# A fused recurrent layer on one core: the first loads of x, the issue of two weights, and fewer warm-up passes

## The chip, the cores and the metric

The kernel runs on one core of a Trainium2 chip. The metric is device time in microseconds (us) from launch to the end of the program; lower is better. Five engines work side by side, each with its own instruction stream: PE (TensorE, matrix products), DVE (VectorE), ACT (ScalarE), POOL (GpSimd) and SP (SyncE, which here only issues DMAs). ACT and POOL issue some DMAs too. DMA transfers run on 16 DMA engines that all issuing engines share.

## The reference

The input x has 8 sequences of 1024 tokens with 256 channels, in float32. Each sequence is normalised and goes through two branches whose results are added to x:

```python
xn = _layernorm(x, axis=-1)
x = x + hawk(xn, Wg, Wi, conv_w, conv_b, lru_Wi, lru_bi, lru_Wg, lru_bg, lam, Wo) \
      + channel_mix(xn, W_r, W_k, W_v, mu_r, mu_k)

def hawk(x, ...):                       # hidden size 384
    gate = x @ Wg.T
    u    = x @ Wi.T
    y    = causal_conv4(u, conv_w) + conv_b
    ig   = sigmoid(y @ lru_Wi.T + lru_bi)
    rg   = sigmoid(y @ lru_Wg.T + lru_bg)
    alpha = exp(-8 * softplus(lam) * rg)
    xbeta = sqrt(1 - alpha**2 + 1e-6) * ig * y
    h    = scan(h = alpha * h + xbeta)   # along the tokens
    return (gelu(gate) * h) @ Wo.T

def channel_mix(x, ...):
    x_prev = shift_one_token(x)
    xr = mu_r * x + (1 - mu_r) * x_prev
    xk = mu_k * x + (1 - mu_k) * x_prev
    return sigmoid(xr @ W_r) * (square(relu(xk @ W_k)) @ W_v)
```

## The kernel before

The sequences are worked one after the other, with the scan and the last product of one sequence laid between the products of the next. Tokens lie 128 to a tile, so a sequence has TT = 8 tiles (`xt`, tokens on partitions). PE needs the normalised x with channels on partitions (`xnT`). Most products use a seven-product scheme of the Strassen kind, for which POOL builds sums of weight blocks (`weight_sum`, line 408: `sum_u`, `sum_r`, `sum_k` and others) and sums of token blocks (`token_sum`, line 803). `w_u` holds two weights side by side, Wi (`"i"`, rows for u) and Wg (`"g"`, rows for the gate); the first sum of `w_u` waits for both.

The order of the instructions on every engine is written out by hand: a list of steps with due times (`PLACES`, `at`, `pe`) is sorted once and issued in that order, and each engine takes its instructions strictly in order. What this case is about is what stands ahead of that list, the head for the first sequence. Tiles of x are treated in four pairs, f = 0 to 3:

- The loads of x are issued by SP, two tiles in each DMA (`load`, line 707). After the second of them stand three instructions of ACT: the DMA of Wi (`load_weight`, line 349), the DMA of the small parameters `par`, and the load of the table for the square root. After the four loads SP issues Wg and the other weights (W_k, W_r, the two of the recurrence, W_v, Wo).
- `busy(15)` (line 1025) gives PE fifteen products of zeros, 128 x 512 in bfloat16, whose results nobody reads. They are first in PE's order. Two more such passes follow the first transposes.
- For each pair, DVE computes the statistics (`bn_stats` line 725, `bn_aggr` line 729); ACT the square root (`deviation`, line 732); DVE a reciprocal and a small product (lines 739 and 740); then ACT normalises one tile of the pair (line 749) and DVE the other (line 747).
- PE transposes the pair (`early_transposes`, line 1044) and ACT copies the result to `xnT` (`early_put`, line 1057). Between the transposes PE computes quarters of the first products with Wi (`plain_quarters`, line 581): per pair f a quarter for each of two output rows, four matmuls of 256 columns each in the records. The order on PE is: passes, transposes 0, two passes, quarter (0, first row), transposes 1, quarter (0, second row), quarter (1, first row), transposes 2, quarters, transposes 3, quarters.
- On ACT the square root of pair 1 stands behind the copy of pair 0, and so on; on DVE the statistics of pair 1 stand behind the normalising of pair 0, and the statistics of pair 2 ahead of the reciprocal of pair 1.

After the quarters come the products of line 415, which belong to the main scheme and to all later sequences.

A DMA's landing is counted on one of eight counters, which the build hands out in turn over the DMAs of SP and ACT. A DMA can be issued only when the one eight places ahead of it has landed. In the kernel before, W_r takes the counter of Wi.

Of the kernel before, what the change touches and what calls it, by code (L numbers as in the profile page):

```python
# [9 lines left out]
AF = mybir.ActivationFunctionType  # L10
# [231 lines left out]
def kernel(  # L242
# [24 lines left out]
    nc = tc.nc  # L267
    B, S, D = x.shape
    TT = S // P
# [6 lines left out]
    def fixed(name, shape, dtype=F32):  # L276
        return const.tile([P] + shape, dtype, tag=name, name=name)


    par = fixed("par", [COLS])  # L280
# [57 lines left out]
    def take():  # L338
        return free.pop(0)

    def give(b):
        free.append(b)
# [4 lines left out]
    def load_weight(engine, name, src):  # L347
        family, first = ROWS[name]
        engine.dma_start(families[family][:, :, first * P : first * P + src.shape[2]], src)
# [356 lines left out]
    def load(s, t, n):  # L706
        nc.sync.dma_start(
            xt[:, t : t + n, :],
            x[s, t * P : (t + n) * P, :].rearrange("(t p) d -> p t d", p=P),
        )  # L710
# [8 lines left out]
    def stats(s, t, n):  # L719
        sums_of_tiles(s, t, n)  # L720
        moments(s, t, n)
# [279 lines left out]
    with tc.manual_schedule():  # L1001
# [1 line left out]
        nc.gpsimd.memset(ln_eps, LN_EPS)  # L1003
        nc.gpsimd.memset(beta_eps, BETA_EPS)
        make_identity(nc, ident)
        for t in range(0, TT, 2):
            load(0, t, 2)
            if t == 2:
                load_weight(nc.scalar, "i", w_i)
                nc.scalar.dma_start(par, params)  # L1010
                nc.scalar.preload_act_table(AF.Sqrt)
        load_weight(nc.sync, "g", w_g)
        load_weight(nc.sync, "k", w_k)
        load_weight(nc.sync, "r", w_r)
        load_weight(nc.sync, "lg", lru_wg)
# [6 lines left out]
        def busy(n):  # L1022
            for _ in range(n):
                b = take()
                nc.tensor.matmul(banks[b], warm[:, 0:P], warm, start=True, stop=True)  # L1025
                give(b)
# [40 lines left out]
                mu_rest, par[:, COL_MU_R : COL_MU_K + DC], -1.0, 1.0, ALU.mult, ALU.add  # L1067
            )

        busy(15)  # L1070
        stats(0, 0, 2)
        scales(0, 2)
        early_normalize(0)
# [289 lines left out]
```

## Time and profile before

| | us |
|---|---|
| median of three runs (620.11 to 620.37) | 620.17 |
| the profiled execution's own time | 620.45 |
| its span, first to last instruction | 618.7 |
| PE busy in the span | 613.3 (99%) |
| DVE, ACT, POOL busy | 532.0, 472.7, 320.2 |
| span's part ahead of the first product of line 415 | 18.2 |

A busy PE is counted from the start of a matmul to its modelled end; matmuls overlap, so the spacing of their starts says how fast they go. Times in the views count from the span's start.

### The profile page before, as it was taken

To read this page: it belongs to the slowest core of one execution; us is meant where nothing else is said; L and a number is where in the kernel's file an instruction comes from. 1 tells how busy PE (TensorE), PEld (TensorE's weight loads), DVE (VectorE), ACT (ScalarE), POOL (GpSimd) and SP (SyncE) were. 2 spreads that over 40 slices of the span, in tenths; PEclk is the share of its full clock that TensorE was granted. 3 is DMA by queue.
4 is the path that set the end of the run, shared out by engine and by line. 5 is a ranking of instruction groups with operands and counts; after the bars stand their busy time and mean duration, and the time that the engine had idled before them with its cause. 6 is when DMAs were issued, how large, how long until landed. Compare 5 with 4: busy or idle time off the path is not lost.

```text
span 618.7 us, 7488 instructions
## 1 busy us (share of the span) xinstructions
PE 613.3 (99%) x2539; PEld 370.0 (60%) x2539; DVE 532.0 (86%) x659; ACT 472.7 (76%) x671; POOL 320.2 (52%) x227
## 2 busy tenths in 40 slices
PE   8999999999999999999999999999999999999998
PEld 4575445954469544794448844497445964457466
DVE  5789799999989798898899888998888986789696
ACT  4988998668894788938889398884888749884880
POOL 4977923579034950549407492084911769427000
DMA  7200600164001810029000480006500044000403
GB/s 272 69 1 8 129 0 1 27 179 69 0 1 48 195 31 0 1 69 205 0 1 1 102 171 0 2 3 151 120 0 1 17 120 69 0 0 1 69 17 119
DMA packets 35478, 35.10 MB, mean 57 GB/s; under 512 B 2800, under 2 KB 34928, under 8 KB 35440
## 3 DMA queue, kind: packets, MB, share of 16 engines
q1 hardware_dynamic: 26416, 25.63, 14.9%
q0 software_dynamic: 8320, 8.39, 9.1%
q10 hardware_dynamic: 704, 0.60, 0.3%
q8 instruction: 20, 0.33, 0.2%
q14 instruction: 18, 0.15, 0.1%
HBM read 19.94 MB, written 8.39 MB: 46 GB/s over the span
## 4 chain that ended last, share of the span: by engine, by line
PE 96%; DVE 3%; issue 0%; ACT 0%; DVEq 0%
PE bank L415 65%; PE bank L421 24%; PE bank L830 4%; PE bank L1025 1%; PE bank L581 1%; DVE xr L820 1%; DVE xt L747 0%; DVE bank L499 0%; DVE st L725 0%; PE bank L754 0%; DVE q L915 0%; PE bank L1044 0%; DVE mv L740 0%; DVE q L930 0%; DVE mv L729 0%
## 5 line engine op out<-in xcount | busy, mean ns | idle before, releaser
L415 PE MATMUL bank<-y,w_l 128*128 128x512 f32 x288 | 138.2, 593 | 0.1
L898 DVE SCALAR_TENSOR_TENSOR y<-u,par,y 128x1024 f32<-128x1024 f32 x72 | 111.6, 1573 | 0.2
L491 ACT COPY bank<-bank 128x512 f32<-128x512 f32 x76 | 43.8, 576 | 61.3 <-PE bank L415 45.3
L415 PEld LDWEIGHTS bank<-y,w_l 128*128 128x128 f32 x288 | 52.9, 190 | 59.2 <-issue 56.9
L499 DVE TENSOR_TENSOR bank<-bank,five 128x512 f32<-128x512 f32 x76 | 52.3, 689 | 26.4 <-PE bank L415 25.6
L415 PE MATMUL bank<-ysum,sum_l 128*128 128x512 f32 x144 | 71.1, 594 | 0.2
L415 PE MATMUL bank<-xsum,sum_u 128*128 128x512 f32 x138 | 69.3, 592 | 0.0
L803 POOL TENSOR_TENSOR tr<-g 128x512 f32<-128x512 f32 x12 | 22.0, 1836 | 83.7 <-ACT u L611 69.8
L803 POOL TENSOR_TENSOR ysum<-y,ysum 128x512 f32<-128x512 f32 x16 | 28.4, 1777 | 53.6 <-DVE y L898 51.1
L803 POOL TENSOR_TENSOR xsum<-ysum 128x512 f32<-128x512 f32 x12 | 16.0, 1347 | 66.0 <-PE bank L421 58.8
L415 PEld LDWEIGHTS bank<-ysum,sum_l 128*128 128x128 f32 x144 | 26.8, 190 | 35.3 <-issue 28.7
L496 ACT COPY five<-bank 128x512 f32<-128x512 f32 x76 | 43.6, 583 | 4.9 <-PE bank L415 2.9
L415 PE MATMUL bank<-xnT,w_u 128*128 128x512 f32 x92 | 47.0, 592 | 0.0
L623 ACT ACTIVATE tr<-bank,half_b 128x512 f32<-128x512 f32 x48 | 32.0, 679 | 15.6 <-PE bank L415 15.6
L415 PEld LDWEIGHTS bank<-xsum,sum_u 128*128 128x128 f32 x138 | 25.7, 190 | 29.7 <-issue 27.5
L421 PE MATMUL bank<-w_o,g 128*128 128x128 f32 x288 | 37.0, 275 | 0.0
L623 ACT ACTIVATE ti<-bank,half_b 128x512 f32<-128x512 f32 x48 | 31.5, 683 | 7.1 <-PE bank L415 6.9
L421 PEld LDWEIGHTS bank<-w_o,g 128*128 128x128 f32 x288 | 35.0, 192 | 2.9 <-issue 2.9
L749 ACT ACTIVATE xt<-xt,mv,std 128x256 f32<-128x256 f32 x60 | 33.9, 596 | 1.5 <-DVE mv L740 1.5
L922 DVE SCALAR_TENSOR_TENSOR ti<-ti,y 128x1024 f32<-128x1024 f32 (+1 forms) x25 | 29.9, 1216 | 3.9 <-ACT ti L623 3.9
L803 POOL TENSOR_TENSOR ysum<-y 128x512 f32<-128x512 f32 x16 | 20.4, 1273 | 23.8 <-DVE y L898 20.1
L925 DVE SCALAR_TENSOR_TENSOR ti<-ti,q 128x1024 f32<-128x1024 f32 (+1 forms) x25 | 31.8, 1272 | 0.7
(165 smaller groups left out, 1480.3 us busy)
## 6 DMA issues: line engine op xcount, KB each, us to landing
side<-in_x_dram POOLq DMA_DIRECT2D x8, 1024.0 KB, 9.3
xt<-in_x_dram SPq DMA_DIRECT2D x28, 256.0 KB, 5.1
xnT<-xk SPq DMA_DIRECT2D x96, 64.0 KB, 2.0
out_dram<-side SPq DMA_DIRECT2D x12, 512.0 KB, 4.8
xt<-in_x_dram SPq DMA_DIRECT2D x1, 1024.0 KB, 5.3
out_dram<-side SPq DMA_DIRECT2D x4, 256.0 KB, 2.2
out_dram<-side SPq DMA_DIRECT2D x6, 128.0 KB, 1.8
w_l<-in_lru_wg_dram SPq DMA_DIRECT2D x1, 576.0 KB, 5.8
```

The source lines that it names most:

```text
L415: nc.tensor.matmul(banks[b], weight, tokens, start=start, stop=True, skip_group_check=True)
L421: nc.tensor.matmul(banks[b][:, p], tokens[:, p], weight, start=start and j == 0, stop=True, skip_group_check=True,)
L491: nc.scalar.copy(banks[bank["B"]], banks[bank["A"]])
L496: nc.scalar.copy(self.five, banks[bank["C"]])
L499: nc.vector.tensor_tensor(banks[bank["C"]], banks[bank["B"]], self.five, ALU.add)
L623: nc.scalar.activation(dst[:, m, HALVES[h]], src, AF.Tanh, bias=half_b[:, b + m : b + m + 1], scale=0.5)
L749: nc.scalar.activation(xa, xa, AF.Identity, bias=m, scale=r)
L803: nc.gpsimd.tensor_tensor(dst[o], a, b, ALU.subtract)
L830: nc.tensor.matmul(banks[b][:, j * D : (j + 1) * D], lhs[:, c, (t + j) * P : (t + j + 1) * P], families[w][:, c, :], start=(j == 0 and c = ...
L898: nc.vector.scalar_tensor_tensor(y[:, m, :], u[:, m, k : k + S], column(COL_CONV_W + k * HC + m), y[:, m, :], ALU.mult, ALU.add,)
L922: nc.vector.scalar_tensor_tensor(ti[:, m, p], ti[:, m, p], 1.0, y[:, m, p], ALU.add, ALU.mult)
L925: nc.vector.scalar_tensor_tensor(ti[:, m, p], ti[:, m, p], 0.5, q[:, m, p], ALU.mult, ALU.mult)
```

## The change

Three edits, all in the head. First, x's tiles 0 and 1 are loaded by one DMA each instead of one for both, and the other three pairs as before, so that SP issues five loads of x in place of four. Second, ACT issues Wi and then Wg, and after them `par` and the table load; SP no longer issues Wg. Third, ten passes of zeros in place of fifteen.

The order of all other instructions on every engine stays as it was. With one DMA more ahead of them, the counters shift: W_k now takes the counter of Wi, W_r that of the load of tile 0.

```diff
@@ -1003,13 +1003,14 @@
         nc.gpsimd.memset(ln_eps, LN_EPS)
         nc.gpsimd.memset(beta_eps, BETA_EPS)
         make_identity(nc, ident)
-        for t in range(0, TT, 2):
+        load(0, 0, 1)
+        load(0, 1, 1)
+        load_weight(nc.scalar, "i", w_i)
+        for t in range(2, TT, 2):
             load(0, t, 2)
-            if t == 2:
-                load_weight(nc.scalar, "i", w_i)
-                nc.scalar.dma_start(par, params)
-                nc.scalar.preload_act_table(AF.Sqrt)
-        load_weight(nc.sync, "g", w_g)
+        load_weight(nc.scalar, "g", w_g)
+        nc.scalar.dma_start(par, params)
+        nc.scalar.preload_act_table(AF.Sqrt)
         load_weight(nc.sync, "k", w_k)
         load_weight(nc.sync, "r", w_r)
         load_weight(nc.sync, "lg", lru_wg)
@@ -1067,7 +1068,7 @@
                 mu_rest, par[:, COL_MU_R : COL_MU_K + DC], -1.0, 1.0, ALU.mult, ALU.add
             )
 
-        busy(15)
+        busy(10)
         stats(0, 0, 2)
         scales(0, 2)
         early_normalize(0)
```

## The prediction

> **What bounds the kernel now.** I read the page's engine shares first, then busy times by stretch, then the chain of waits over the first 19 us, then the DMA answers and the engines' rows there. By stretch (length, then busy time of PE, PEld, DVE, ACT, POOL):
>
> ```profile
> 18.20:107.00 88.80, 88.65 (x295) 47.56 (x294) 78.39 (x114) 80.78 (x117) 59.54 (x45) 1.00 0.16 33
> 107.00:152.00 45.00, 44.75 (x233) 29.97 (x232) 43.43 (x53) 31.50 (x46) 33.05 (x21) 1.00 0.43 94
> 152.00:610.00 458.00, 458.00 (x1926) 278.21 (x1925) 397.51 (x456) 350.79 (x493) 218.04 (x140) 1.00 0.23 49
> ```
>
> From 18.2 us on PE is idle for 0.4 of 591.8 us. The change touches nothing there, so its worth is the shift of the first product of line 415, which starts at 18.19. The chain ahead of it (start, length, what):
>
> ```profile
> 1.18 5.96 PE bank L1025 x15
> 7.14 0.45 PE bank L1044 x4
> ...
> 8.10 0.31 ACT std L732
> ...
> 8.82 0.98 DVE xt L747
> ...
> 10.70 0.94 DVE mv L740
> ...
> 11.79 1.06 DVE xt L747
> 12.85 0.04 issue
> 12.90 0.55 PE bank L1044 x3
> 13.44 1.81 PE bank L581 x8
> ```
>
> The fifteen passes hold the first transposes, whose copy stands on ACT ahead of pair 1's square root at 8.10. From there the chain is DVE's normalising of pairs 1 and 2; from 12.90 PE never waits again. Those DVE steps are long for a reason that their neighbours show:
>
> ```profile
> 5.02 0.16 DVE L740 SCALAR_TENSOR_TENSOR mv<-mv,std 128x2 f32<-128x2 f32 x1
> 5.22 0.41 DVE L747 TENSOR_SCALAR xt<-xt,std,mv 128x256 f32<-128x256 f32 x1
> 8.65 2.01 POOL L408 TENSOR_TENSOR sum_u<-w_u 128x384 f32<-128x384 f32 x2 [7.21 <-DMA w_u<-in_w_g_dram]
> ```
>
> L740 takes 0.16 and L747 0.41 with POOL idle, but 0.94 and 0.98 to 1.06 while POOL's sums of w_u run (8.65 to 12.7, four of 1.0 each): DVE's step ends about where POOL's does. POOL starts when Wg lands.
>
> **The loads of x and the weights.** DMA queues between 3.0 and 3.7 us (q1 is SP's, q10 ACT's; packets, MB, share), and three issues (KB, us to landing) of Wi at 0.73, of x's second pair at 1.23, of Wg at 2.75:
>
> ```profile
> q10 hardware_dynamic: 159, 0.24, 101.1%
> q1 hardware_dynamic: 3, 0.00, 0.2%
> ...
> w_u<-in_w_i_dram ACTq DMA_DIRECT2D x1, 384.0 KB, 4.5
> xt<-in_x_dram SPq DMA_DIRECT2D x1, 256.0 KB, 4.7
> w_u<-in_w_g_dram SPq DMA_DIRECT2D x1, 384.0 KB, 5.8
> ```
>
> The DMA engines are full. Though x's second pair was issued at 1.23, only Wi moves: the first pair, then Wi, then the second pair. Whether this is turn-taking between the queues or order of issue, the changed kernel's order comes out the same: tile 0, Wi, tile 1, Wg, pair 1, par, pair 2, pair 3. The rate: from Wi's landing (0.73 + 4.5 = 5.2) to Wg's (2.75 + 5.8 = 8.5), 1166 KB (three pairs, par, Wg) in 3.3 us, 353 KB/us. I count bytes from Wi's landing, with 640 KB before it:
>
> - tile 1 completes the same 640 KB: 5.2; before, both tiles were there at 0.73 + 2.7 = 3.4;
> - Wg, 1024 KB: 6.3 (before 8.5); pair 1, 1280 KB: 7.0 (before 5.9); pair 2, 1550 KB: 7.8 (6.7); pair 3, 1806 KB: 8.5 (7.4).
>
> The Trainium skill's page DMA: Bandwidth & Descriptors, section Issuing engines are not separate DMA queues, speaks against the change: it says that DMAs from different issuers share the same engines and interleave, so a second issuer saves only issue time. By it Wg on ACT takes its time from x, as counted here; a reader who instead thinks of ACT's queue as separate would get pair 1 at its old 5.9.
>
> Issuing itself: SP has one load more (0.5 us; four took 1.98) and is rid of Wg (0.69). W_k must now wait for Wi's landing (4.9) instead of going at 3.48; W_r, the recurrence's weights, W_v and Wo stand behind it, W_v besides for Wg, Wo for pair 2. The engines have x and Wg to move until 8.5 anyway, so W_k and W_r land as before, near 9.2 and 9.9; POOL reads them after 10.5. ACT's Wg issue (0.65, like Wi's) pushes par to 2.1 and the 1.28 us table load to 2.75 to 4.03; the first square root comes later than that (4.49 before, 5.9 below). Cost of both: nothing.
>
> **Pair 0.** Before, statistics began at 3.42 and the square root came 1.07 later. With tile 0's done (0.37), it is 0.70 after 5.2: 5.9. As before, +0.33 to the reciprocal and +0.20 to L740: 6.45. POOL starts 0.15 after Wg: also 6.45, with sums of w_u to 10.5. No row shows which goes first when they start together. If DVE does, only L747 is held: pair 0 is ready at 7.5. If POOL does, L740 ends at 7.4, and L747, which follows behind a new sum, at 8.5. Before it was 5.82. I take 8.5, by the row at 10.70, where POOL was 0.08 ahead and DVE waited; 7.5 is the other end.
>
> **Pairs 1 and 2.** Statistics of pair 1 follow on DVE at 8.5; square root 1.07 later, 9.6, also behind pair 0's copy (9.0 to 9.55). L740 at 10.1 waits for POOL's fourth sum to 10.4; L747 then meets POOL's short sums of W_r and W_k (0.45 each) and ends at 11.0. Before it was 9.80. With pair 0 at 7.5: square root 8.6, L740 held to 9.45, L747 to 10.5. Pair 2: from 9.80 to 12.84 was 3.04, 1.49 of them waiting for POOL (0.78 in L740, 0.71 in L747); with short sums I put 0.4: 11.0 + 1.95 = 12.95.
>
> **PE.** From pair 1's readiness: transposes done 0.45 later, two quarters of 0.86, then transposes 2 of 0.44. Before: 9.80 to 11.97, then idle 0.93, and done at 13.28. Changed: 11.0 + 0.45 + 1.72 = 13.17, where pair 2 (12.95) is ready, done at 13.61: **0.33 later**. With pair 1 at 10.5: 13.11, 0.17 earlier. So most of pair 1's lateness goes into PE's old idle time, and the five passes removed (2.1 us) gain nothing, since PE then waits for x: what is late next is tile 1. POOL's first sum over xnT, which waited 0.70 for the last copy, moves with PE.
>
> **The speed of PE.** The passes of the first 5.8 us, and four late ones (count; duration min/median/max in ns; first and last start):
>
> ```profile
> L1025 PE MATMUL bank<-five x11: 606/634/634, 1.2 to 5.4; 128*128 128x512 bf16 x11
> ...
> L1025 PE MATMUL bank<-five x4: 379/379/380, 6.5 to 7.6; 128*128 128x512 bf16 x4
> ```
>
> Starts are 0.43 apart at first (1.58, 2.01, ... 5.85) and 0.22 after 6.5, with the granted clock at 1.00 throughout: PE doubles its speed at about 6.4, after 5.2 us of unbroken work. Ten passes end at 1.18 + 4.27 = 5.45, and PE then idles until about 8. No row shows whether it will have doubled. At one end it has: nothing. At the other it starts afresh at 8.1 and needs 5.2 us again, to 13.3: transposes, passes and the quarter take double, to 11.6; transposes 1 to 12.45; the next quarter (1.71) is half done at 13.3 and ends at 13.73; a quarter, 14.6; transposes 2, 15.03: 1.75 later than before. I take nothing, since 4.3 us is nearer to 5.2 than to none, and the five zero-passes need not be the deciding ones.
>
> The Trainium skill's TensorE: Matmul & The Clock Gate, section Part 1, puts the change near 4 us of sustained work, decided by a free-running window of 3.4 us, so that it varies by run. By it ten passes mostly suffice and the sum stays at +0.33; this trace's 5.2 us is longer than its figure.
>
> **Sum.** 620.45 (profiled execution) + 0.33 = 620.78. That execution is 0.28 above the median of the runs, so against the median: **620.5**. What a measurement of this kernel can tell from no change is about 0.2%, 1.24 us.
>
> **Rivals.**
>
> 1. PE is still slow when the transposes come. Place: transposes 0 to quarter (1, first row). Price 1.75: 620.17 + 1.75 = 621.9, slower. It decides once the doubling comes later than about 12.3, as each us of dense slow work costs half. For: 4.27 is less than the 5.2 shown, which is why its chance is large. Against: one trace's 5.2 may hold a wait for a fixed moment. If the doubling comes 2 us later still, 622.9.
> 2. Tile 1 goes before Wi. Both tiles land at 3.4 as before, pair 0 is ready at 5.5 with tile 0's statistics done early, and the passes end there. But pair 1 lands at 7.0: square root 8.1, as in the profile, L740 at 8.6 held by POOL to 9.45, L747 to 10.3; PE 10.3 + 2.17 + 0.44 = 12.9, 0.4 earlier: 619.8. For: single loads have half the packets and may be quicker to issue. Against: the window above, where x issued at 1.23 waited for Wi.
> 3. x keeps ahead of the weights altogether. Pair 1 at 5.9, square root at 7.0, no POOL in the way: pair 1 ready at 8.2, pair 2 by 10.4; transposes 2 done at 10.8: 2.4 earlier, 617.8. Against: the full DMA engines and Wi's turn.
>
> **How the numbers follow.** Forecast 0.49 (620.0 to 621.1: the ends -0.17 and +0.33, and some 0.3 of timing), rival 1 0.28, rival 2 0.17, rival 3 0.06. The range 619.6 to 622.2 takes in rival 2 and rival 1 at its price, and leaves out rival 3 and the dearest of rival 1. Faster by 0.2% is rival 3 alone, 0.06. Slower is nearly all of rival 1 and a little of the forecast's upper end, 0.28. The rest is 0.66.
>
> **What would show it.** In the changed profile: Wi's packets ahead of tile 1's, tile 1's statistics near 5.2, POOL's first sum near 6.45, pair 1 ready near 11.0, the first product of line 415 near 18.5, and quarters with starts 0.22 apart. Starts 0.43 apart there mean rival 1; statistics of tile 1 near 3.5, rival 2; pair 1's statistics at 5.9, rival 3. Wrong it would be if POOL's sums hold DVE longer than a sum each, or if the weights come so late that POOL, not PE, starts the main stage.

## The result

| | kernel before | changed kernel |
|---|---|---|
| median (12 runs each, same chip), us | 620.31 (618.94 to 620.58) | 620.83 (620.40 to 622.64) |
| ratio to the kernel before | | 1.0018, 95% interval 1.0011 to 1.0025 |
| profiled execution, us | 620.45 | 621.15 |
| its span, us | 618.7 | 619.4 |
| first product of line 415 starts at, us | 18.19 | 18.91 |

The change made the kernel a little slower, 0.5 us by the medians and 0.18% (1.1 us) by the ratio, which is within what I called no change. (Three of the twelve runs of the kernel before lie near 619, none of the changed kernel's, so that the means lie 1.0 us apart.) The profiled executions differ by 0.7 us, and put all of it ahead of the first product of line 415, which comes 0.7 us later. Later on PE is as full as before: the stretch from 152 to 610 us has 458.00 us of PE work in both.

The chain of waits of the changed kernel up to the last quarters (start, length, what). The same places of before stand in the prediction.

```profile
1.18 4.45 PE bank L1026 x10
5.63 1.65 issue
7.28 0.65 PE bank L1045 x4
...
7.95 0.59 ACT xnT L1058
...
8.59 1.77 PE bank L581 x4
10.35 1.17 PE bank L1045 x4
11.53 2.20 PE bank L581 x8
13.72 0.44 PE bank L1045 x4
14.16 1.80 PE bank L581 x8
```

Ten passes end at 5.63, and PE is idle for 1.65 until pair 0 is there. DVE's normalising of pairs 1 and 2, which made up the chain before, has gone from it: from 8.59 on it is PE all through. But PE is slow there. Eight matmuls of the quarters took 1.81 us from 13.44 in the kernel before, and here 1.80 from 14.16; the four from 8.59 take 1.77, twice as much each.

The clock that the throttle granted to PE says the same. Busy time by stretch of the changed kernel (length, then PE, PEld, DVE, ACT, POOL; the last three numbers are the granted clock, the DMA engines' share and GB/s):

```profile
1.20:5.50 4.30, 4.30 (x10) 1.31 (x10) 0.82 (x3) 1.28 (x1) 0.24 (x3) 1.00 0.84 250
5.50:8.90 3.40, 1.51 (x8) 0.89 (x8) 2.30 (x12) 1.78 (x4) 1.39 (x2) 1.00 1.04 347
8.90:12.30 3.40, 3.40 (x11) 2.31 (x10) 3.29 (x13) 1.63 (x4) 3.32 (x6) 0.51 1.05 377
12.30:18.90 6.60, 6.60 (x35) 5.52 (x34) 2.01 (x7) 4.96 (x9) 3.98 (x9) 1.00 0.42 144
```

PE got fast at 5.5, was busy for 1.51 of the next 3.40 us, and then ran at half the clock for 3.4 us, just when it had work without a gap. (The first stretch reads 1.00 although the passes' starts are 0.43 apart there: the first, slow stretch of a program is not in this number.) Of the twelve runs, eight show a mean granted clock of 0.995 or 0.997; 0.997 is what one such stretch makes (0.5 x 3.4 / 619 = 0.0027).

The other four runs, at 1.000, are no faster: 620.40, 620.60, 620.99 and 622.07, median 620.80, against 620.62 to 622.64, median 620.83, for the eight. So the stretch explains what the profiled execution did; that it makes the difference between the two kernels over all runs is not shown. (A run at 1.000 may also have got fast late, since the first slow stretch is not in the number; none was profiled.)

DVE's rows of the changed kernel (start, length, operation, and in brackets the idle time before it), for the terms of the prediction:

```profile
2.93 0.43 DVE L725 BATCH_NORM_STATS2 st<-xt 128x6 f32<-128x256 f32 x1 [1.81 <-DMA xt<-in_x_dram]
5.11 0.43 DVE L725 BATCH_NORM_STATS2 st<-xt 128x6 f32<-128x256 f32 x1 [1.75 <-DMA xt<-in_x_dram]
...
6.58 0.41 DVE L747 TENSOR_SCALAR xt<-xt,std,mv 128x256 f32<-128x256 f32 x1
7.59 0.75 DVE L725 BATCH_NORM_STATS2 st<-xt 128x6 f32<-128x256 f32 x2 [0.60 <-DMA xt<-in_x_dram]
...
9.51 1.05 DVE L747 TENSOR_SCALAR xt<-xt,std,mv 128x256 f32<-128x256 f32 x1
```

and POOL's row, its first two sums of w_u:

```profile
7.51 1.95 POOL L408 TENSOR_TENSOR sum_u<-w_u 128x384 f32<-128x384 f32 x2 [6.07 <-DMA w_u<-in_w_g_dram]
```

Tile 0's statistics come at 2.93, tile 1's only at 5.11; pair 1's wait for their load to 7.59; POOL starts at 7.51, so pair 0's L747 (0.41) meets no sum and pair 1's (1.05) does.

### The profile page after: what moved, and what is told of

It is laid out like the page before. It is cut to its first block, busy times and chain, and to the rows that moved or that the text cites. A ratio compares the mean times of both kernels' runs of the same rounds, so it can differ in the third digit from the quotient of the medians.

```text
span 619.4 us, 7479 instructions
## 1 busy us (share of the span) xinstructions
PE 612.9 (99%) x2534; PEld 370.5 (60%) x2534; DVE 530.5 (86%) x659; ACT 472.5 (76%) x671; POOL 320.2 (52%) x227
## 4 chain that ended last, share of the span: by engine, by line
PE 97%; DVE 2%; issue 1%; ACT 0%; DVEq 0%
PE bank L415 65%; PE bank L421 24%; PE bank L830 4%; PE bank L581 1%; PE bank L1026 1%; DVE xr L820 1%; PE bank L1045 0%; DVE bank L499 0%; PE bank L754 0%; DVE q L915 0%; DVE st L725 0%; DVE q L930 0%; DVE g L507 0%; DVE bank L507 0%; ACT xnT L1058 0%
```

## The experiments

Each kernel was compared with runs of the kernel before on its own chip. Theory A, from the profile above: the loss is the half-speed stretch, which an idle stretch of PE brings on, and the idle stretch comes from late loads of x. Theory B: late loads cost by themselves, through the chain. Medians of different rows may come from different chips, so the ratios compare better. The change has three parts, so the experiments take them apart (the six combinations besides the two kernels were run), and then test the causes.

| passes | tiles 0, 1 | Wg | label | median us | ratio to before, 95% interval |
|---|---|---|---|---|---|
| 15 | pair | SP | the kernel before | 620.0 to 620.3 | |
| 10 | pair | SP | e2 | 619.45 | 0.9995 (0.9987 to 1.0004) |
| 15 | single | SP | e4 | 620.57 | 1.0013 (1.0004 to 1.0022) |
| 15 | pair | ACT | e3, e11 | 622.32, 620.94 | 1.0039 (1.0025 to 1.0053), 1.0024 (1.0012 to 1.0036) |
| 10 | single | SP | e5 | 620.88 | 1.0015 (1.0006 to 1.0023) |
| 10 | pair | ACT | e6 | 620.38 | 1.0008 (0.9999 to 1.0017) |
| 15 | single | ACT | e1 | 620.57 | 1.0011 (1.0002 to 1.0019) |
| 10 | single | ACT | the changed kernel | 620.83 | 1.0018 (1.0011 to 1.0025) |

### Fifteen passes in the changed kernel (e1)

```diff
-        busy(10)
+        busy(15)
```

> The changed kernel with fifteen passes. Theory A (the loss is PE's half speed from 8.9 to 12.3 us, which the gap between the passes and the late transposes 0 brought on): the passes reach to about 7.3, where the transposes start anyway, PE stays fast, transposes 2 end near 13.1 as against 14.0, the first product of line 415 starts near 18.1; about 0.7 us faster than the changed kernel, within 0.2 us of the kernel before. Theory B (the loss is the later landing of x alone): the first product of line 415 stays near 18.9 and the time as in the changed kernel, 0.5 us above the kernel before.

Measured: 620.57, against 620.83 for the changed kernel. No run of eleven shows a half-speed stretch (granted clock 1.000 in all). In its profiled execution PE's matmuls are fast throughout:

```profile
5.90:9.30 3.40, 2.64 (x13) 1.21 (x12) 2.98 (x10) 1.67 (x4) 2.78 (x3) 1.00 1.07 367
9.30:12.70 3.40, 3.04 (x15) 2.10 (x14) 3.03 (x11) 2.24 (x5) 3.32 (x8) 1.00 1.05 382
```

The first product of line 415 starts at 18.30 and not 18.91, near theory A's 18.1; the span is 618.8 in place of 619.4. So the passes do keep PE fast, and the profiled pair differs by 0.6 us. Over the runs theory A did not hold: with no half speed at all the kernel is still 0.4 us above the kernel before (ratio 1.0011, interval 1.0002 to 1.0019) where theory A allowed 0.2, and theory B's 0.5 is nearer. Against the changed kernel the medians differ by 0.3 and the intervals overlap, so what the half speed costs over many runs is not settled, and late loads cost something without it.

The two profiled executions differ in one more thing. POOL's first sum, which waits for Wg, starts at 6.52 here and at 7.51 in the changed kernel, though the DMAs are issued in the same order. It is the meeting of DVE and POOL for which the prediction found no row:

```profile
6.43 0.16 DVE L740 SCALAR_TENSOR_TENSOR mv<-mv,std 128x2 f32<-128x2 f32 x1
6.63 1.04 DVE L747 TENSOR_SCALAR xt<-xt,std,mv 128x256 f32<-128x256 f32 x1
6.52 2.01 POOL L408 TENSOR_TENSOR sum_u<-w_u 128x384 f32<-128x384 f32 x2 [5.08 <-DMA w_u<-in_w_g_dram]
```

DVE's L740 starts 0.09 us ahead of POOL and keeps its 0.16; L747 is held to 1.04, and pair 0 is ready at 7.7, near the prediction's "other end" of 7.5.

### Ten, then twelve passes in the kernel before (e2, e10)

```diff
-        busy(15)
+        busy(10)     # e2; 12 in e10
```

> The kernel before with ten passes and nothing else changed. Theory A: pair 0 is ready at 5.8, so PE idles only 0.3 us after the passes, gets fast near 5.5 to 6.5 and stays so; transposes 0 end at 6.5, the copy at 7.1, pair 1's square root comes at 7.05 to 7.1 in place of 8.10, DVE normalises pair 1 before POOL's first sum (8.65), pair 1 is ready at 8.2 to 8.4 and transposes 2 end at 11.1 to 11.5 as against 13.3: 1.8 to 2.1 us faster than before, 618.3. Rival (ten passes are too few whatever follows): PE is at half speed until 9 to 12 us, quarters take 1.7 in place of 0.86, and the time is within 0.6 us of the kernel before or above it.

> The kernel before with twelve passes: slow passes end at 6.3, some 0.5 behind pair 0 (5.8). If the passes alone hold transposes 0: 619.5 to 619.8, between ten (619.45) and fifteen (620.2). If the gain of ten passes is chance of one comparison: 620.1 to 620.3, as before.

Measured: 619.45 with ten, 619.25 with twelve (ratio 0.9991, interval 0.9982 to 1.0000, against 620.02). In the profiled executions the rival, that ten passes are too few whatever follows, is out: behind the ten, eight matmuls of the quarters take 1.80 us, as they do at full speed before. Chance is not out: by the medians ten passes gain 0.7 us and twelve 0.8, by the ratios 0.3 and 0.6, and the interval of ten takes in no change while that of twelve just reaches it. The chain of the kernel with twelve:

```profile
1.18 4.83 PE bank L1025 x12
6.01 0.56 PE bank L1044 x4
...
7.07 0.31 ACT std L732
...
7.79 0.41 DVE xt L747
...
9.10 0.97 DVE mv L740
...
10.22 0.94 DVE xt L747
11.16 0.04 issue
11.21 0.55 PE bank L1044 x3
```

Transposes 0 at 6.0 instead of 7.1, pair 1's L747 at its short 0.41 because it comes ahead of POOL's sums, transposes 2 at 11.2 instead of 12.9. The first product of line 415 starts at 16.50, 1.7 us earlier than before (with ten passes 16.88, 1.3 earlier), but the spans are only 1.4 and 1.0 us shorter. Theory A's 1.8 to 2.1 us (618.3) was too much: the profiled head gains less, and some 0.3 us of it is given back later. POOL, which waited 0.70 us for xnT before, now goes from its sums of the weights straight to those of the tokens.

By the medians this is the best of all the kernels tried, though its interval against the kernel before just reaches 1: it is the kernel before with three passes fewer.

### Single loads alone, and with ten passes (e4, e5)

```diff
+        load(0, 0, 1)
+        load(0, 1, 1)
+        load_weight(nc.scalar, "i", w_i)
+        nc.scalar.dma_start(par, params)
+        nc.scalar.preload_act_table(AF.Sqrt)
-        for t in range(0, TT, 2):
+        for t in range(2, TT, 2):
             load(0, t, 2)
-            if t == 2:
-                load_weight(nc.scalar, "i", w_i)
-                nc.scalar.dma_start(par, params)
-                nc.scalar.preload_act_table(AF.Sqrt)
...
-        busy(15)     # e5 only
+        busy(10)     # e5 only
```

> The kernel before with tiles 0 and 1 loaded singly and nothing else: Wi stands between them as in the changed kernel, Wg stays with SP, fifteen passes. If tile 1 lands behind Wi (5.1 as in the changed kernel): pair 0 ready at 7.1, just as the passes end, pair 1's statistics at 7.1, its square root near 8.1 as before: within 0.2 us of the kernel before, that is, the single loads cost nothing while fifteen passes cover them. Rival (the single loads are the loss): statistics of pair 0 push everything behind them by 1.3 us, of which 0.4 to 0.9 us reaches the end.

> Tiles 0 and 1 singly and ten passes; Wg stays with SP. Theory A' (the single loads put tile 1 behind Wi, and what that costs is PE's idle time between the passes and transposes 0; PE falls to half speed when a stretch of 3.4 us after it got fast is busy for less than some 40%): transposes 0 at about 7.0 as with fifteen passes, a stretch from 5.5 to 8.9 about 45% busy, so mostly fast: within 0.3 us of the same kernel with fifteen passes (620.6), now and then 1 to 2 us above it with a granted clock of 0.997. Rival (fewer passes gain by themselves, as in the kernel before, which with ten ran at 619.45): 619.5 to 619.9.

Measured: 620.57 and 620.88. Tile 1 does land behind Wi (statistics of tile 1 at 4.86 with fifteen passes). In the profiled execution of e4 the first product of line 415 starts at 18.02, no later than before, so the expectation held for that execution; over eleven runs it is 0.4 above the kernel before, more than the 0.2 I allowed and within what the rival named. No run of e4 is below a granted clock of 0.999, so this cost isn't half speed; as in e1, late data cost something by themselves, which speaks for theory B. It shows in runs that are missing: of the 29 runs of the kernel before on that chip 11 lie below 619.7, of the 22 of e4 and e1 none (the lowest is 619.71).

Fewer passes, worth 0.7 by the medians in the kernel before, gain nothing once tile 1 is late: e5 is 0.6 above the kernel before on its chip, e4 0.4 on its own, with overlapping intervals, and seven of e5's eleven runs show a granted clock of 0.994 or 0.997. Its profiled execution:

```profile
4.30:7.70 3.40, 1.47 (x10) 0.69 (x7) 2.39 (x11) 0.95 (x3) 0.00 (x0) 1.00 1.08 366
7.70:11.10 3.40, 3.33 (x11) 2.34 (x10) 3.04 (x11) 1.62 (x4) 2.31 (x3) 0.51 1.04 373
```

Again 1.5 us of work in 3.4, then 3.4 at half speed. I had expected mostly runs at full clock; the limit of some 40% in theory A' was too low, for 1.47 of 3.4 is 43%, and the 1.51 of the changed kernel was 44%. Nor does one stretch cost 1 to 2 us here: the six runs at 0.997 lie from 620.50 to 621.03, the four at 0.999 or 1.000 from 620.52 to 620.91. Only the run at 0.994, two stretches' worth, is far off, at 622.33.

### Wg on ACT alone (e3, e11), with ten passes (e6), and with PE's idle time filled (e7)

```diff
         for t in range(0, TT, 2):
             load(0, t, 2)
             if t == 2:
                 load_weight(nc.scalar, "i", w_i)
+                load_weight(nc.scalar, "g", w_g)
                 nc.scalar.dma_start(par, params)
                 nc.scalar.preload_act_table(AF.Sqrt)
-        load_weight(nc.sync, "g", w_g)
...
-        busy(15)     # e6 only
+        busy(10)     # e6 only
...
                     quarters(f, 0)
+                    if f == 0:
+                        pe(busy, 6, length=0)     # e7 only
```

> The kernel before with Wg issued by ACT behind Wi; pairs of x and fifteen passes as before. By the turn-taking of the queues: pair 1 lands at 5.9 as before, Wg near 7.0 in place of 8.5, pairs 2 and 3 near 7.8 and 8.5. Statistics of pair 2 end at 8.5 and hold pair 1's reciprocal by 0.15; POOL's sums start near 7.1, hold L747 to 10.1, and are done by 11.1, so pair 2 meets short sums: transposes 2 end at 12.7 in place of 13.28, 0.4 to 0.6 us faster than before. Rival (Wg goes ahead of pair 1): pair 1 at 7.0, pair 1's square root still at 8.1, POOL from 6.5 to 10.5; between 0.3 faster and 0.2 slower.

> Wg issued by ACT, fifteen passes, as measured once at 622.3, with a granted clock of 0.997 in four of six runs but 1.000 in the profiled one. If half speed is what costs the 2 us: runs at 0.997 again lie near 622 to 623 and runs at 1.000 near 620.3, and a profiled run at 0.997 shows matmul starts 0.43 apart for 3.4 us somewhere between 8 and 15 us, behind PE's idle stretch before transposes 1. If data lateness is what costs it: runs near 622 at 1.000 as well.

> Wg issued by ACT and ten passes; pairs of x as before. Theory A': pair 2's statistics wait for their load to about 8.6, DVE does them ahead of pair 1's reciprocal, pair 1 is ready near 10.7 whatever the passes; PE idles from 8.6 to 10.4 and again falls to half speed in many runs: 621 to 623, as with fifteen passes (622.3). Rival (the fifteen passes brought that loss about by holding transposes 0): 619.5 to 620.3.

> Wg issued by ACT with fifteen passes, and six more passes of zeros on PE behind quarter (0, first row), where it idled from 8.66 to 10.36. They do nothing for the output. Theory A' (the 2 us above the kernel before come from PE's half speed after an idle stretch, not from the data's lateness): the granted clock stays at 1.000 in all runs and the time comes down from 622.3 to 620.2 to 620.6. Rival (the lateness itself costs the 2 us): 622.0 or more, as the passes can only add.

Measured: 622.32 (e3, six runs) and 620.94 (e11, the same kernel, twelve runs); 620.38 with ten passes; 620.85 with the filling passes (ratio 1.0013, interval 1.0004 to 1.0022). The expectation of e3, a gain, was wrong. What happens in the data shows on DVE in e11:

```profile
6.42 0.30 DVE L729 BATCH_NORM_AGGREGATE mv<-st 128x2 f32<-128x6 f32 x2
8.66 0.75 DVE L725 BATCH_NORM_STATS2 st<-xt 128x6 f32<-128x256 f32 x2 [1.94 <-DMA xt<-in_x_dram]
9.33 0.15 DVE L739 RECIPROCAL std<-std 128x2 f32<-128x2 f32 x1
9.51 0.95 DVE L740 SCALAR_TENSOR_TENSOR mv<-mv,std 128x2 f32<-128x2 f32 x1
10.50 1.05 DVE L747 TENSOR_SCALAR xt<-xt,std,mv 128x256 f32<-128x256 f32 x1
```

Wg comes in turn ahead of pair 2. Pair 2's statistics stand on DVE ahead of pair 1's reciprocal and wait for that load to 8.66; pair 1's own data were long there. Then POOL's sums hold both of pair 1's steps, and PE is idle from 9.5 to 11.2.

The runs of e11 fall apart by the granted clock: five at 0.997 with 622.26 to 622.75, seven at 0.999 or 1.000 with 619.89 to 621.46. Half speed thus goes with 2 us more, as expected. Hardly all of that is the clock: 3.4 us at half the clock do the work of 1.7 us, so one stretch delays PE by 1.7 us at most, and the medians of the two groups (622.37 and 620.24) are 2.1 apart. The lateness without half speed costs little in most runs; the one at 621.46 is the profiled one, in which PE got fast late, at 6.7. With the six filling passes all eleven runs are at 0.999 or 1.000 and none is above 621.42, where e3 and e11 had nine of eighteen at 622 or more. That supports the cause for these runs: work that does nothing takes them away. The median came down to 620.85 only, not to the 620.2 to 620.6 that theory A' named, and it is above e11's seven runs without half speed.

The expectation of e6 failed: no run of eleven shows the half-speed stretch, though PE idles for 2.4 us in its profiled execution, longer than in e11's (1.6). The median, 620.38, is just above what the rival named. The profiled executions give a bound (e3, e6 and e11):

```profile
8.65:12.05 3.40, 1.81 (x10) 1.19 (x9) 3.29 (x14) 1.62 (x4) 3.32 (x4) 1.00 1.05 386
...
6.50:9.90 3.40, 2.00 (x10) 1.04 (x8) 1.35 (x6) 0.78 (x2) 1.42 (x2) 1.00 1.04 370
9.90:13.30 3.40, 2.04 (x10) 1.57 (x11) 3.33 (x11) 1.87 (x4) 3.32 (x6) 1.00 1.07 392
...
10.10:13.50 3.40, 2.22 (x11) 1.72 (x12) 3.28 (x11) 2.04 (x5) 3.32 (x6) 1.00 1.05 384
```

PE's busy time in the 3.4 us from when PE got fast (or the 3.4 after), and what followed: 1.51 (changed kernel) and 1.47 (e5), half speed; 1.81 (e3), 2.00 and 2.04 (e6), 2.22 (e11), 2.64 (e1), full speed. So the limit lies between 1.5 and 1.8 of 3.4 us as this profile counts busy time. Why Wg on ACT falls below it in half of the runs with fifteen passes and in none with ten stays open: no execution of that kernel at 0.997 was profiled. The 1.81 of e3 is close to the limit, and the 3.4 us are counted from the moment PE got fast, which was 5.2 in e3 and 6.7 in e11; a shift of that moment may decide, but this is argued, not shown.

### Wi behind the tiles (e8), Wg ahead of pair 3 (e9)

```diff
-        for t in range(0, TT, 2):              # e8, with busy(10)
+        load(0, 0, 1)
+        load(0, 1, 1)
+        load_weight(nc.sync, "i", w_i)
+        for t in range(2, TT, 2):
             load(0, t, 2)
-            if t == 2:
-                load_weight(nc.scalar, "i", w_i)
-                nc.scalar.dma_start(par, params)
-                nc.scalar.preload_act_table(AF.Sqrt)
+        nc.scalar.dma_start(par, params)
+        nc.scalar.preload_act_table(AF.Sqrt)
...
         for t in range(0, TT, 2):              # e9, with busy(10)
+            if t == 6:
+                load_weight(nc.sync, "g", w_g)
             load(0, t, 2)
...
-        load_weight(nc.sync, "g", w_g)         # e9
```

> Tiles 0 and 1 singly, then Wi, all issued by SP, then the other pairs and Wg, with ten passes; ACT issues par alone. If order of issue decides: both tiles land by 3.2 to 3.4, pair 0 is ready at 5.3 to 5.6 as the passes end, pair 1 lands near 5.9 as before, POOL starts at 8.4 as before; pair 1 is ready at 7.8, transposes 2 end at 10.9 to 11.5: 619.0 or below, 1.1 us faster than the kernel before and faster than the kernel before with ten passes. Rival (what single loads cost is their number, not Wi's place): 620.2 to 620.6, as with the single loads alone.

> The kernel before with ten passes and Wg issued by SP ahead of pair 3 in place of behind it. Theory A'' (with ten passes the next bound is POOL, whose sums of w_u, w_r and w_k end only at 15.35, so that the sums over tokens start late; pair 3 has 1 us to spare): Wg lands near 7.1, pair 3 near 8.2, POOL is through with the weights at 14.2 and waits for xnT again, pair 1's normalising meets POOL and costs 0.6 to 0.8, pair 2's less; about as the kernel before with ten passes (619.45) or 0.3 us below it. Rival (POOL isn't bound; its sums only hold DVE): 0.5 us above the kernel before with ten passes, 619.9.

Measured: e8 620.56 (619.53 to 623.61; ratio 1.0014, interval 1.0002 to 1.0026), e9 619.61 (1.0001, 0.9992 to 1.0010). The expectation of e8, 619.0 or below, failed, and its time is what the rival named. In the profiled execution the head of e8 does mostly what I expected: both tiles' statistics begin at 2.81, transposes 2 at 11.3, the first product of line 415 at 16.68, 1.5 us earlier than before. And then PE waits:

```profile
17.67 1.39 POOL sum_r L408
19.06 0.41 POOL sum_k L408
19.47 1.24 POOL xsum L803
20.71 0.04 issue
20.75 14.84 PE bank L415 x30
```

In this execution, the slowest of twelve, Wg landed so late that POOL started at 10.41 (expected: 8.4), and the token sums that PE needs came at 20.7. PE's 3.0 us of idle time then brought a half-speed stretch from 21.5 to 24.9 (granted clock 0.50). So the rival's mechanism is not what this execution shows; the other runs, at 619.53 to 622.75, were not profiled. What it does show is what can limit a faster head: POOL's sums of the weights, 9 us here from 10.41 to the first token sum, 7 in the kernel before. In e9, where Wg comes 0.6 us earlier than with ten passes alone, POOL waits for xnT again (0.85 us), but its sums hold pair 1, transposes 2 start at 12.1, and the time is no better than e2's; it lies between what the expectation (619.45 or 0.3 below) and its rival (619.9) named, and settles neither. Earlier Wg pays on POOL and costs on DVE.

## Why the prediction was right, and where its steps were not

The range (619.6 to 622.2) and the largest chance (no change) held; forecast 620.5 from 620.17, measured 620.83 from 620.31. That the number came so near is in part luck, as the steps show; their times are those of one profiled execution:

- **All of it lies ahead of line 415's first product.** Right for the changed kernel. As a general step, that an earlier head goes through to the end, it is wrong: e10 gave back part and e8's profiled execution more than all.
- **Order of the DMAs.** Right: tile 1 behind Wi, at 5.1 (forecast 5.2). The later ones came later than the single rate gave: Wg at 1.41 + 6.0 = 7.4 (forecast 6.3), pair 1 at 7.5 (7.0). The rate was not far off, but it leaves out the stragglers: of the sixteen landing signals of Wg in the trace thirteen have come by 6.09 and the last comes at 7.36. In e1, with the same order, the last comes at 6.37.
- **Pair 0.** I took 8.5, with POOL first; it was 7.2 (ACT's tile; DVE's 7.0). The step that failed is POOL's start at 6.45; it came at 7.51, since Wg was later. The other end, 7.5, was the nearer; where the two did meet (e1), DVE went first.
- **Pair 1.** Forecast 11.0, other end 10.5; L747 ended at 10.56, held by POOL's third sum (9.42 to 10.41; 1.05 instead of 0.41). L740, which the prediction held as well, took 0.18 at 9.30. So the other end's number came out, by one wait in place of two.
- **PE from there.** By the prediction's addition 10.56 + 0.45 + 1.72 + 0.44 = 13.17, 0.11 earlier than before. The quarter behind transposes 2 in fact started at 14.00 in place of 13.28.
- **The speed of PE.** This is the step that failed: "I take nothing". PE did get fast during the ten passes, at 5.5, so rival 1 as I put it (still slow) is wrong as well; it fell back at 8.9 after 1.5 us of work in 3.4. What the stretch costs I estimate from the two rows at 14.00 - 13.17 = 0.8 us, less than rival 1's 1.75, because part of the slow work would have waited anyway. The forecast's +0.33 from late data and the +0.7 of the profiled execution are thus made of different terms: -0.1 from the chain and +0.8 from the clock. This holds for that execution. Over the runs the half speed is not shown to be what the change costs: the changed kernel's runs without it are as slow, and e1 and e4, which have none, are 0.4 above the kernel before. There late data are part of the cost, and how the two share it stays open.
- **The five passes gain nothing.** Right, but for the reason named only together with tile 1's lateness: with tile 1 on time ten passes are 0.7 us faster by the medians and 0.3 by the ratio, whose interval takes in no change (e2).
- **Rival 2** (tile 1 before Wi) did not occur. **Rival 3**'s price, 2.4 us, left out POOL, which had 0.70 us to spare before its first sum over tokens; e8 shows what that comes to.

The Trainium skill's DMA: Bandwidth & Descriptors, section Issuing engines are not separate DMA queues, agrees with the runs: Wg on ACT moved x's later pairs back (the statistics of pair 2 wait for their load to 8.66 in e11; in the kernel before they ran at 6.85 without a wait). Its TensorE: Matmul & The Clock Gate, section Why this matters for your kernels, puts the fall to half speed behind gaps of about 3 us; in the changed kernel the longest gap was 1.65 us, and the fall came all the same. There the measurement decides.

## What to carry to other kernels

Passes that keep PE busy should last until the data come, and little longer. In the profiles here fifteen held the transposes to 7.1 where twelve let them start at 6.0, and ten with later data left PE idle long enough to fall to half speed; in the medians twelve did best, by a margin that these runs don't quite settle. A weight moved to a second issuing engine still takes its turn on the same DMA engines, so count bytes in order of issue against what is needed first. Late data cost 0.4 us here even where PE kept its speed. And price a faster head at the engine that is next in line, here POOL with 0.70 us to spare, before adding it to the end.

## What I had not expected of the hardware

PE falls back to half speed without any long gap: 1.47 and 1.51 us of work in a stretch of 3.4 us were followed by 3.4 us at a granted clock of 0.51, 1.81 and more were not, and the longest gaps there were 1.93 and 1.65 us. When PE first gets fast differs between executions of kernels whose first ten passes are the same, from 4.3 us (e5) to 6.7 us (e11), though it began its work at 1.18 in all. With fifteen passes that moves transposes 0 between 6.3 us (e7, fast at 4.9) and 7.1 us (e11, fast at 6.7). This may be why runs of the kernel before lie in two groups, near 619.3 and 620.2, and why a kernel whose data come late has no run in the lower group; neither was tested.
